# Four stacked graph layers on one core: weight sums moved to VectorE, and a new order of work in the first and the last group

## The chip, the cores and the metric

The kernel runs on one core of a Trainium2 chip. The metric is device time in microseconds (us), the median of three runs: 2460.32 us before the change (2459.33 to 2461.46). The profile is one further execution of the same kernel, with a span of 2456.7 us.

Engines are named as in the profile: PE is TensorE (matmul) and PEld its weight loads, DVE is VectorE, ACT is ScalarE, POOL is GpSimd, SP is SyncE, which here issues every transfer.

## The reference, cut to what matters

There are 128 graphs of 128 nodes with 512 features each, in 32-bit floats. Four layers follow each other, and each ends in a residual addition and a layer norm over the features:

```python
x = layernorm(x + relu(An @ x @ K0 + b0))                        # An = d^-1/2 (A + I) d^-1/2
x = layernorm(x + softmax_nodes(sum_m(q k^T / 8 * A)) * (x @ Wv^T))
x = layernorm(x + relu(concat(x, (A @ x) / deg) @ W2^T))
x = layernorm(x + An @ (x @ W3 + b3))
```

Every layer therefore has a product of a 128 x 512 matrix with one or two 512 x 512 weights for each graph, and layers 0, 2 and 3 have an aggregation with the graph's 128 x 128 matrix as well.

## The kernel before, in words

**Tiling.** The 128 graphs are worked on in 32 groups of G = 4. In a group the graphs form pairs: q is the pair (0 or 1) and r is the row in the pair, so graph 2q + r. Two graphs stacked, r = 0 over r = 1, form the left operand of a 2 x 2 block product whose right operand is a weight, also cut into 2 x 2 blocks. The product is done in Strassen-Winograd form with seven block products instead of eight. They are named B11, T1, B21, B22, T2, T3 and T4 (line 30). `project` (line 526) runs them in the order B11, B21, T1, T2, B22, T3; T4 is a "tail" that is put off until the next product's B11 has run (`finish_tails`, line 522). For some layers B21 comes after T1 (`early=False`).

**Sums ahead of the products.** T1 to T4 need sums of blocks. For a weight they are made once in the program (`weight_sums`, line 372: four operations of 128 x 512). For a left operand they are made for each group (`left_sums`, line 503: four operations named s1, s2, a21 and s4 below, on GpSimd as a rule). B11, B21 read blocks as they are. B22 reads s4, T1 reads s1, T2 reads s2, T3 the changed a21.

**Accumulation.** B11 and B21 share one PSUM region (g), T1 and B22 another (q), T2, T3 and T4 a third (v). When a second product is added onto a region, it must wait until the reader of the first is done: B21 waits for ScalarE's copy of B11 (`s_o`), B22 waits for VectorE's `u5 = q + sb` (written `u_o` in the profile).

**Transposes and aggregates.** `aggregate` (line 465) multiplies the features of one graph with the turned adjacency (four matmuls into a PSUM tile p_agg), and ScalarE copies the result out as the left operand. The normalised x of a layer is turned for the next product either through DRAM (`turn_x`, middle groups) or on TensorE (`turn_on_tensor`, line 489, for the first and last groups: a ScalarE copy, four transposes p_xT, a ScalarE copy back). `prep_rows` (line 411) scales the adjacency on VectorE; `prep_transpose` (line 436) turns it on TensorE for groups 0 and 1, and `prep_turn` (line 447) through DRAM for the rest.

**Order of the work.** The program is recorded first and then put in order by a planner (`Plan.schedule`, line 197). TensorE's order is the order of recording, exactly. On all other engines an instruction's place follows from a due time (the latest time at which TensorE's order needs it, counted backwards) and from estimated durations (`estimate`, line 292). What is recorded where, through `hooks` that run behind a named product, so sets TensorE's order directly and the other engines' order through the due times. At run time each engine works through its queue in order.

`begin` (line 847) writes out the first groups by hand: adjacency of group 0, layer 0 of groups 0 and 1, layer 1 of both, layer 2 of group 0, and so on. The loop at line 881 then interleaves layer 0 and 1 of group t with layer 2 and 3 of group t - 1. From line 898 on the last group's layers 2 and 3 are done pair by pair.

**Norms.** `norm_stats` (line 622) takes mean and variance with VectorE's batch-norm statistics, then GpSimd raises the variance to the power -1/2 and makes the products, and ScalarE applies scale and shift. `norm_last` (line 601) is the same for layer 3 with ScalarE doing the sums; only the very last row (last group, r = 1, pair 1) takes `norm_stats`. Each normalised graph of the last group is stored by a transfer of its own.

Of the kernel before, what the change touches and what calls it, by code (L numbers as in the profile page):

```python
# [10 lines left out]
FP = mybir.dt.float32  # L11
AF = mybir.ActivationFunctionType
ALU = mybir.AluOpType
AX = mybir.AxisListType

P = 128
K = 32
Q = P // K
G = 4
F = 512  # L20
# [291 lines left out]
def kernel(  # L312
# [59 lines left out]
    def weight_sums(w, eng):  # L372
        eng.tensor_tensor(w[:, :, T3], w[:, :, B22], w[:, :, T1], ALU.subtract)
        eng.tensor_tensor(w[:, :, T1], w[:, :, T1], w[:, :, B11], ALU.subtract)
        eng.tensor_tensor(w[:, :, T2], w[:, :, B22], w[:, :, T1], ALU.subtract)
        eng.tensor_tensor(w[:, :, T4], w[:, :, B21], w[:, :, T2], ALU.subtract)
# [59 lines left out]
    def prep_transpose(t):  # L436

        anT, arT, ana, d = prep_tiles(t)
        for i, done in ((0, lambda p: nc.vector.tensor_tensor(anT, p, per_graph(d), ALU.mult)),
                        (1, lambda p: nc.scalar.copy(arT, p))):  # L440
            p = ps_t.tile([P, G, P], FP, tag="pt", name=f"p_a{i}_{t}")
            with nc.unit():
                for g in range(G):
                    nc.tensor.transpose(p[:, g, :], ana[:, i, g, :], ident)
            done(p)
# [155 lines left out]
    def norm_last(name, t, r, pairs):  # L601

        z = st["x", t]
        qs = slice(pairs[0], pairs[-1] + 1)
        sm, nm, sq, rstd, nmr = (sp.tile([P, 2], FP, tag=f"last{i}", name=f"last{i}_{t}_{r}", bufs=2) for i in range(5))
        for q in pairs:
            row = tp.tile([P, F], FP, tag="row", name=f"row_{t}_{r}_{q}", bufs=1)
            nc.scalar.activation(row, z[:, 2 * q + r, :], AF.Copy, accum_out=sm[:, q:q + 1])
        nc.scalar.mul(nm[:, qs], sm[:, qs], -1.0 / F)
        for q in pairs:  # L610
            row = tp.tile([P, F], FP, tag="row", name=f"square_{t}_{r}_{q}", bufs=1)
            nc.scalar.activation(row, z[:, 2 * q + r, :], AF.Square, bias=nm[:, q:q + 1], accum_out=sq[:, q:q + 1])
        nc.gpsimd.tensor_scalar(rstd[:, qs], sq[:, qs], 1.0 / F, LN_EPS, ALU.mult, ALU.add)
        nc.gpsimd.tensor_tensor(rstd[:, qs], rstd[:, qs], nhalf[:, qs], ALU.pow)
        nc.gpsimd.tensor_tensor(nmr[:, qs], nm[:, qs], rstd[:, qs], ALU.mult)
        for q in pairs:
            zg = z[:, 2 * q + r, :]
            nc.scalar.activation(zg, zg, AF.Identity, bias=nmr[:, q:q + 1], scale=rstd[:, q:q + 1])
            if t == last:
                nc.sync.dma_start(out[t * G + 2 * q + r], zg)  # L620

    def norm_stats(name, t, r, pairs):
        if name == "o3" and (t, r, pairs[-1]) != (last, 1, 1):
            return norm_last(name, t, r, pairs)
        z = st["x", t]
        qs = slice(pairs[0], pairs[-1] + 1)
        mv = sp.tile([P, 2, 2], FP, tag="mv", name=f"mv{name}_{t}_{r}")
        for q in pairs:
            s = sp.tile([P, 6], FP, tag="bn", name=f"bn{name}_{t}_{r}_{q}")
            nc.vector.bn_stats(s, z[:, 2 * q + r, :])  # L630
            nc.vector.bn_aggr(mv[:, q, :], s)
        rstd = sp.tile([P, 2], FP, tag="rstd", name=f"rstd{name}_{t}_{r}")
        mr = sp.tile([P, 2], FP, tag="mr", name=f"mr{name}_{t}_{r}")
        nmr = sp.tile([P, 2], FP, tag="nmr", name=f"nmr{name}_{t}_{r}")
        nc.gpsimd.tensor_scalar(rstd[:, qs], mv[:, qs, 1], LN_EPS, None, ALU.add)
        nc.gpsimd.tensor_tensor(rstd[:, qs], rstd[:, qs], nhalf[:, qs], ALU.pow)
        nc.gpsimd.tensor_tensor(mr[:, qs], mv[:, qs, 0], rstd[:, qs], ALU.mult)
        nc.scalar.mul(nmr[:, qs], mr[:, qs], -1.0)
        for q in pairs:
            zg = z[:, 2 * q + r, :]  # L640
            nc.scalar.activation(zg, zg, AF.Identity, bias=nmr[:, q:q + 1], scale=rstd[:, q:q + 1])
            if name == "o3":
                nc.sync.dma_start(out[t * G + 2 * q + r], zg)


    def l0_agg(t, eng=nc.gpsimd, pairs=(slice(0, 2),)):
        left("agg0", t)
        for g in range(G):
            aggregate("agg0", t, g, st["anT", t])
        left_sums("agg0", t, eng, pairs)  # L650
# [7 lines left out]
    def l0_out(t, hooks=None, pairs=(0, 1)):  # L658
        fin = relu_add(t, pairs)

        def bias(h):
            return b0_sb[:, None, h * H:(h + 1) * H].to_broadcast([P, len(pairs), H])

        def first(p, block):
            sa, sb = copy_first(p, block)[0], block("sb")
            nc.gpsimd.tensor_tensor(sb, sa, bias(1), ALU.add)
            nc.gpsimd.tensor_tensor(sa, sa, bias(0), ALU.add)
            return sa, sb

        def c11(p, block):  # L670
            c = block("u2")
            nc.vector.tensor_tensor(c, p, bias(0), ALU.add)
            fin(0, 0, c)

        project("o0", t, [("agg0", w0_sb)], first, c11, fin, hooks, pairs=pairs)
# [111 lines left out]
    def l2_agg(t, r):  # L787
        if r == 0:
            left("agg2", t)
        for g in (r, 2 + r):  # L790
            aggregate("agg2", t, g, st["arT", t])
        if r == 1:
            left_sums("agg2", t)

    def l2_both(t, r):

        if r == 0:
            left("xT2", t)
            left("agg2", t)
        for g in (r, 2 + r):  # L800
            aggregate("agg2", t, g, st["arT", t])
        turn_on_tensor("xT2", t, r)
        if r == 1:
            left_sums("xT2", t, nc.vector)
            left_sums("agg2", t, nc.vector)

    def l2_out(t, hooks=None, pairs=(0, 1)):
        fin = relu_add(t, pairs)
        project("o2", t, [("xT2", w2x_sb), ("agg2", w2a_sb)],
                copy_first, lambda p, b: fin(0, 0, p), fin, hooks, pairs=pairs)  # L810
# [8 lines left out]
    def l3_agg_pair(t, q, eng):  # L819
        left(f"agg3{q}", t)  # L820
        for g in (2 * q, 2 * q + 1):
            aggregate(f"agg3{q}", t, g, st["anT", t])
        left_sums(f"agg3{q}", t, eng, ONE_BY_ONE[q:q + 1])
# [23 lines left out]
    def begin():  # L847

        prep_rows(0)
        prep_transpose(0)  # L850
        weight_sums(w0_sb, nc.gpsimd)
        l0_agg(0, nc.vector, ONE_BY_ONE)
        prep_rows(1)
        l0_out(0, {B21: [lambda: prep_transpose(1)], B22: [lambda: l0_agg(1)]})
        weight_sums(wv_sb, nc.vector)
        for w in (w2x_sb, w2a_sb, w3_sb):
            weight_sums(w, nc.gpsimd)

        l0_out(1)
        l1_turn(0, turn_on_tensor, (0,))  # L860
        finish_tails()
        l1_turn(0, turn_on_tensor, (1,))
        l1_out(0, {T3: [lambda: l1_turn(1, turn_on_tensor)]})
        l1_out(1, {B11: [lambda: l1_scores(0)], T1: [lambda: l1_softmax(0)], B21: [lambda: l1_add(0)]})
        l2_both(0, 0)
        l2_out(0, {B21: [lambda: l2_both(0, 1), lambda: prep(2)], T2: [lambda: l1_scores(1)], B22: [lambda: l1_softmax(1)], T3: [lambda: l1_add(1)]})
        l0_agg(2)
        l2_turn(1)
        l0_out(2, {B21: [lambda: l2_agg(1, 0)], T1: [lambda: l2_agg(1, 1)]})
        l3_agg(0)  # L870
        l3_bias(0)
        l3_out(0)

    def prep(t):
        if t < NT:
            load(t)
            prep_rows(t)
            prep_turn(t)

    begin()  # L880
    for t in range(2, NT):
        u = t - 1
        if t > 2:
            l0_out(t, {B21: [lambda: l2_agg(u, 0)], T1: [lambda: l2_agg(u, 1)]})
        tails.append(lambda: l1_turn(t))
        prep(t + 1)
        l2_out(u)
        if t < last:
            l0_agg(t + 1)
        l1_out(t, {})  # L890
        l3_agg(u)
        l1_scores(t)
        l3_bias(u)
        l3_out(u, {B11: [lambda: l1_softmax(t)], B21: [lambda: l1_add(t)]})
        if t < last:
            l2_turn(t)
# [1 line left out]
    l2_both(last, 0)  # L898
    held = tails.pop()
    for q in range(2):  # L900
        l2_out(last, {B21: [lambda: l2_both(last, 1), held]} if q == 0 else {}, (q,))
    for q in range(2):
        l3_agg_pair(last, q, nc.gpsimd)
        l3_bias(last, (2 * q, 2 * q + 1))
        l3_out(last, None, f"agg3{q}", (q,))
    finish_tails()
# [32 lines left out]
```

## Time and profile before

| what | value |
|---|---|
| device time, median of 3 | 2460.32 us |
| span of the profile | 2456.7 us |
| PE busy | 2436.3 us (99%) |
| DVE, POOL, ACT busy | 1711.2, 1341.0, 994.7 us |
| one middle group | 75.49 us of PE work |
| TensorE's granted clock | 0.999 |
| bytes read and written | 126.62 and 112.20 MB, 97 GB/s |

All instructions of the kernel carry line 271, since a recorder issues them; groups are told apart by their tiles. `p_o` is the PSUM of a projection, `p_v` of layer 1's product, `p_agg` of an aggregation, `p_xT` of a transpose of x, `p_a` of the adjacency. `w_sb` is the weight of layer 0 or of layer 3, `w2x_sb` and `w2a_sb` the two halves of layer 2's. A name with an s behind it (`agg0s`, `xT2s`, `agg30s`) is a left sum. `s_o` and `u_o` are blocks on their way from PSUM to x. `rstdo`, `mro`, `nmro` and `last` are the small columns of a norm.

In a timeline's line the first number is the start in us from the span's start, the second the time from there to the end of the last of the merged instructions. The bracket is how long the engine was idle before, and what ended that. In the list of waits the three numbers are the total in us, the count and the longest. Not all idle time of an engine costs something: here it is TensorE's idle time that does, and the time behind its last product.

### The profile page before, as it was taken

To read this page: it belongs to the slowest core of one execution; us is meant where nothing else is said; L and a number is where in the kernel's file an instruction comes from. 1 tells how busy PE (TensorE), PEld (TensorE's weight loads), DVE (VectorE), ACT (ScalarE), POOL (GpSimd) and SP (SyncE) were. 2 spreads that over 40 slices of the span, in tenths; PEclk is the share of its full clock that TensorE was granted. 3 is DMA by queue.
4 is the path that set the end of the run, shared out by engine and by line. 5 is a ranking of instruction groups with operands and counts; after the bars stand their busy time and mean duration, and the time that the engine had idled before them with its cause. 6 is when DMAs were issued, how large, how long until landed. Compare 5 with 4: busy or idle time off the path is not lost.

```text
span 2456.7 us, 35481 instructions
## 1 busy us (share of the span) xinstructions
PE 2436.3 (99%) x12462; PEld 2091.5 (85%) x12462; DVE 1711.2 (70%) x3389; ACT 994.7 (40%) x2120; POOL 1341.0 (55%) x1586
## 2 busy tenths in 40 slices
PE   8999999999999999999999999999999999999998
PEld 7788888888888888888888888888888888888887
DVE  6676776767667677676776667767677676776665
ACT  3344334444334443344433444433444334444335
POOL 6365555546455565555555554645555555555443
PEclk9999999999999999999999999999999999999999
DMA  5143243442434424244332444334443334432320
GB/s 176 27 124 85 76 107 108 124 111 61 113 90 125 125 68 109 74 127 122 86 91 83 124 116 108 71 101 103 116 125 72 88 90 125 125 99 64 82 70 35
DMA packets 393265, 241.14 MB, mean 98 GB/s; under 512 B 140416, under 2 KB 358016, under 8 KB 393088
## 3 DMA queue, kind: packets, MB, share of 16 engines
q1 hardware_dynamic: 393088, 238.88, 36.5%
q8 instruction: 99, 1.62, 0.3%
q14 instruction: 78, 0.64, 0.1%
HBM read 126.62 MB, written 112.20 MB: 97 GB/s over the span
## 4 chain that ended last, share of the span: by engine, by line
PE 97%; DVE 1%; ACT 1%; POOL 0%; DMA 0%; issue 0%; SPq 0%; ACTq 0%; POOLq 0%; DVEq 0%
PE p_o L271 62%; PE p_v L271 20%; PE p_agg L271 14%; PE p_sc L271 1%; DMA ana<-in_adj_dram 0%; DVE agg0s L271 0%; PE p_ws L271 0%; DVE x L271 0%; PE p_xT L271 0%; ACT xT L271 0%; PE p_w L271 0%; DVE ana L271 0%; ACT x L271 0%; DVE u_o L271 0%; SPq L271 0%
## 5 line engine op out<-in xcount | busy, mean ns | idle before, releaser
L271 PE MATMUL p_o<-w_sb,agg 128*128 128x256 f32 x2048 | 471.5, 380 | 1.6 <-DVE u_o L271 0.9
L271 PEld LDWEIGHTS p_o<-w_sb,agg 128*128 128x128 f32 x2048 | 386.4, 190 | 53.2 <-ACT s_o L271 1.1
L271 ACT COPY agg<-p_agg 128x512 f32<-128x512 f32 (+1 forms) x415 | 222.9, 552 | 456.2 <-PE p_agg L271 456.2
L271 PE MATMUL p_v<-wv_sb,xT 128*128 128x320 f32 x1024 | 291.4, 433 | 0.0
L271 DVE TENSOR_TENSOR v<-p_v,v 128x320 f32<-128x320 f32 x316 | 154.7, 490 | 173.1 <-PE p_v L271 170.6
L271 PE MATMUL p_o<-w2x_sb,xT 128*128 128x256 f32 x1024 | 263.3, 380 | 1.7 <-ACT s_o L271 1.1
L271 PE MATMUL p_o<-w2a_sb,agg 128*128 128x256 f32 x1024 | 262.9, 379 | 0.0
L271 PEld LDWEIGHTS p_v<-wv_sb,xT 128*128 128x128 f32 x1024 | 192.3, 190 | 75.8 <-issue 0.2
L271 PEld LDWEIGHTS p_agg<-anT,x 128*128 128x128 f32 x2048 | 238.7, 192 | 7.0 <-DVE anT L271 0.6
L271 PE MATMUL p_agg<-anT,x 128*128 128x128 f32 x2048 | 239.4, 275 | 0.3 <-DVE anT L271 0.3
L271 POOL TENSOR_TENSOR xT1s<-xT 128x512 f32<-128x512 f32 x32 | 45.5, 1423 | 351.1 <-DVE xT L271 250.0
L271 PEld LDWEIGHTS p_o<-w2x_sb,xT 128*128 128x128 f32 x1024 | 194.4, 190 | 32.4 <-ACT s_o L271 1.9
L271 PE MATMUL p_v<-wv_sb,xT1s 128*128 128x320 f32 x768 | 217.5, 433 | 0.1
L271 PEld LDWEIGHTS p_o<-w2a_sb,agg 128*128 128x128 f32 x1024 | 194.8, 190 | 26.1
L271 DVE TENSOR_TENSOR u_o<-p_o,u_o 128x512 f32<-128x512 f32 (+1 forms) x196 | 131.1, 670 | 118.2 <-PE p_o L271 118.1
L271 ACT ACTIVATE x<-x,nmro,rstdo 128x512 f32<-128x512 f32 x257 | 197.5, 808 | 4.5
L271 PE MATMUL p_o<-w2x_sb,xT2s 128*128 128x256 f32 x768 | 197.4, 380 | 1.5 <-DVE xT2s L271 1.5
L271 PE MATMUL p_o<-w2a_sb,agg2s 128*128 128x256 f32 x768 | 197.2, 379 | 0.0
L271 PEld LDWEIGHTS p_v<-wv_sb,xT1s 128*128 128x128 f32 x768 | 145.8, 190 | 57.5 <-POOL xT1s L271 0.6
L271 PE MATMUL p_o<-w_sb,agg0s 128*128 128x256 f32 x768 | 177.2, 380 | 3.5 <-DVE u_o L271 2.7
L271 PE MATMUL p_o<-w_sb,agg3s 128*128 128x256 f32 x744 | 173.9, 384 | 0.0
L271 DVE BATCH_NORM_STATS2 bno<-x 128x6 f32<-128x512 f32 x257 | 167.8, 683 | 3.4
(143 smaller groups left out, 4258.8 us busy)
## 6 DMA issues: line engine op xcount, KB each, us to landing
x<-in_x_dram SPq DMA_DIRECT2D x31, 1024.0 KB, 5.6
out_dram<-x SPq DMA_DIRECT2D x31, 1024.0 KB, 5.2
xT2s<-x SPq DMA_DIRECT2D x120, 256.0 KB, 2.5
xT2y<-xT2s SPq DMA_DIRECT2D x240, 128.0 KB, 3.3
xT1s<-x SPq DMA_DIRECT2D x120, 256.0 KB, 2.6
xT1y<-xT1s SPq DMA_DIRECT2D x240, 128.0 KB, 3.2
sa<-ana SPq DMA_DIRECT2D x120, 128.0 KB, 3.4
ya<-sa SPq DMA_DIRECT2D x120, 128.0 KB, 3.3
```

The costliest lines, as they stand in the source:

```text
L271: getattr(getattr(self.nc, op.engine), method)(*[v.real() if isinstance(v, Ref) else v for v in args], **{k: v.real() if isinstance(v, Ref ...
```

## The change

It has five parts.

1. The sums of layer 0's weight are made on VectorE instead of GpSimd.
2. In group 0's layer 0 the transposes of the second adjacency follow B11 instead of B21.
3. In group 0 and in the last group the second rows' aggregates and turned x for layer 2 follow that product's B11 instead of its B21, so that B21 stands between them and T1, which needs their sums. In the 29 middle groups (t > 2) the two halves of layer 2's aggregates each follow one product later of layer 0. Attention scores and softmax of group 1 are recorded one product sooner.
4. Pair 0's aggregates of the last layer 3 are recorded behind B22 of pair 1's layer 2, ahead of its T3, instead of after the whole product.
5. The last pair's normalisation is done on VectorE as (x - mean) x rstd, without the products that ScalarE's form needs, and the very last statistics are taken in two halves, the half that is finished first ahead.

```diff
@@ norm_last
-        nc.gpsimd.tensor_tensor(nmr[:, qs], nm[:, qs], rstd[:, qs], ALU.mult)
+        if (t, pairs[0]) != (last, 1):
+            nc.gpsimd.tensor_tensor(nmr[:, qs], nm[:, qs], rstd[:, qs], ALU.mult)
         for q in pairs:
             zg = z[:, 2 * q + r, :]
-            nc.scalar.activation(zg, zg, AF.Identity, bias=nmr[:, q:q + 1], scale=rstd[:, q:q + 1])
+            if (t, q) == (last, 1):
+                nc.vector.tensor_scalar(zg, zg, nm[:, q:q + 1], rstd[:, q:q + 1], ALU.add, ALU.mult)
+            else:
+                nc.scalar.activation(zg, zg, AF.Identity, bias=nmr[:, q:q + 1], scale=rstd[:, q:q + 1])
@@ norm_stats
         for q in pairs:
-            s = sp.tile([P, 6], FP, tag="bn", name=f"bn{name}_{t}_{r}_{q}")
-            nc.vector.bn_stats(s, z[:, 2 * q + r, :])
+            n = 2 if name == "o3" else 1
+            s = sp.tile([P, n, 6], FP, tag="bn", name=f"bn{name}_{t}_{r}_{q}")
+            for h in reversed(range(n)):
+                nc.vector.bn_stats(s[:, h], z[:, 2 * q + r, h * (F // n):(h + 1) * (F // n)])
             nc.vector.bn_aggr(mv[:, q, :], s)
...
         nc.gpsimd.tensor_tensor(rstd[:, qs], rstd[:, qs], nhalf[:, qs], ALU.pow)
+        if name == "o3":
+            zg = z[:, G - 1]
+            nc.vector.tensor_scalar(zg, zg, mv[:, 1, 0:1], rstd[:, 1:2], ALU.subtract, ALU.mult)
+            nc.sync.dma_start(out[B - 1], zg)
+            return
@@ begin
-        weight_sums(w0_sb, nc.gpsimd)
+        weight_sums(w0_sb, nc.vector)
         l0_agg(0, nc.vector, ONE_BY_ONE)
         prep_rows(1)
-        l0_out(0, {B21: [lambda: prep_transpose(1)], B22: [lambda: l0_agg(1)]})
+        l0_out(0, {B11: [lambda: prep_transpose(1)], B22: [lambda: l0_agg(1)]})
...
         l2_both(0, 0)
-        l2_out(0, {B21: [lambda: l2_both(0, 1), lambda: prep(2)], T2: [lambda: l1_scores(1)], B22: [lambda: l1_softmax(1)], T3: [lambda: l1_add(1)]})
+        l2_out(0, {B11: [lambda: l2_both(0, 1), lambda: prep(2)], T1: [lambda: l1_scores(1)], T2: [lambda: l1_softmax(1)], T3: [lambda: l1_add(1)]})
@@ the loop over groups
-            l0_out(t, {B21: [lambda: l2_agg(u, 0)], T1: [lambda: l2_agg(u, 1)]})
+            l0_out(t, {T1: [lambda: l2_agg(u, 0)], T2: [lambda: l2_agg(u, 1)]})
@@ the last group
-        l2_out(last, {B21: [lambda: l2_both(last, 1), held]} if q == 0 else {}, (q,))
+        l2_out(last, {B11: [lambda: l2_both(last, 1)], B21: [held]} if q == 0 else {B22: [lambda: l3_agg_pair(last, 0, nc.gpsimd)]}, (q,))
     for q in range(2):
-        l3_agg_pair(last, q, nc.gpsimd)
+        if q == 1:
+            l3_agg_pair(last, 1, nc.gpsimd)
```

More of the change, by code (lines that the diff above doesn't have):

```diff
@@ L641, in norm_stats @@
             nc.scalar.activation(zg, zg, AF.Identity, bias=nmr[:, q:q + 1], scale=rstd[:, q:q + 1])
-            if name == "o3":
-                nc.sync.dma_start(out[t * G + 2 * q + r], zg)
     def l0_agg(t, eng=nc.gpsimd, pairs=(slice(0, 2),)):
```

## The prediction

> **What bounds the kernel now.** I read the page's busy times first, then TensorE's waits, then the timelines of the stretches in which those waits lie. The page:
>
> ```profile
> PE 2436.3 (99%) x12462; PEld 2091.5 (85%) x12462; DVE 1711.2 (70%) x3389; ACT 994.7 (40%) x2120; POOL 1341.0 (55%) x1586
> ```
>
> TensorE is idle for 2456.7 - 2436.3 = 20.4 us of the span. The change alters no matmul in count or shape, so 20.4 us is all that it can win; a gain must come out of named gaps. TensorE's waits over the whole span:
>
> ```profile
> PE p_o L271 <- DVE u_o L271: 3.6, 3, 2.7
> PE p_o L271 <- ACT s_o L271: 1.8, 3, 0.7
> PE p_o L271 <- DVE xT2s L271: 1.5, 1, 1.5
> ...
> PE p_o L271 <- POOL agg30s L271: 1.3, 1, 1.3
> PE p_xT L271 <- ACT xT1y L271: 1.0, 1, 1.0
> PE p_o L271 <- DVE agg0s L271: 0.8, 3, 0.4
> ```
>
> With four smaller rows these make 12.3 us; the same view cut to 400 to 2300 us has no row at all, so the middle groups run without a gap, 75.49 us each in the chain. The other 7.9 us are the tail: TensorE ends at 2448.8. Where the waits lie, in TensorE's timeline (brackets: idle before, and who ended it; one more, 0.46 behind s_o, is at 2403.5):
>
> ```profile
> 15.17 2.00 PE L271 MATMUL p_o<-w_sb,agg 128*128 128x256 f32 x8 [0.68 <-ACT s_o L271]
> ...
> 25.97 1.99 PE L271 MATMUL p_o<-w_sb,agg0s 128*128 128x256 f32 x8 [2.74 <-DVE u_o L271]
> ...
> 91.25 1.13 PE L271 MATMUL p_o<-w2x_sb,xT 128*128 128x256 f32 x4 [0.68 <-ACT s_o L271]
> ...
> 99.13 1.13 PE L271 MATMUL p_o<-w2x_sb,xT2s 128*128 128x256 f32 x4 [1.50 <-DVE xT2s L271]
> ...
> 2437.30 1.13 PE L271 MATMUL p_o<-w_sb,agg30s 128*128 128x256 f32 x4 [1.31 <-POOL agg30s L271]
> ```
>
> In the first 26 us the late engine is VectorE. Its timeline, between GpSimd's weight sums and the addition that frees B22's bank:
>
> ```profile
> 12.99 1.75 DVE L271 TENSOR_TENSOR ana<-ana,d 128x512 f32<-128x512 f32 x1 [0.62 <-POOL d L271]
> ...
> 16.34 2.90 DVE L271 TENSOR_TENSOR agg0s<-agg 128x256 f32<-128x256 f32 x2
> ...
> 21.97 0.75 DVE L271 TENSOR_TENSOR agg0s<-agg,agg0s 128x256 f32<-128x256 f32 x2
> ...
> 25.23 1.28 DVE L271 TENSOR_TENSOR u_o<-p_o,sb_o 128x512 f32<-128x512 f32 x2
> ```
>
> ```profile
> 12.92 4.62 POOL L271 TENSOR_TENSOR w_sb<-w_sb 128x512 f32<-128x512 f32 x3
> ```
>
> See that two 256-wide additions take 2.90 us while GpSimd adds and 0.75 us as soon as it stops (21.8).
>
> [...] 1.45 us for one 256-wide addition beside GpSimd, 0.37 alone. [...]
>
> **Part A, the start.** w0's four sums leave GpSimd and become four 512-wide VectorE additions, 0.61 us from start to start (xT2s and agg2s at 2409.7 to 2412.1). The transposes of the second adjacency come behind B11 and not B21, 0.9 us of TensorE work that can lie under the 0.68 wait. Addressed: 0.68 + 0.22 + 0.37 + 0.21 (the three agg0s waits) + 2.74 = 4.22 us.
> VectorE from 12.99 on[...]: two row scalings 1.3, weight sums 4 x 0.61 = 2.4, six agg0s additions of 0.34 = 2.0, anT 0.6, the freeing addition 0.6: 6.9, so it would end at 19.9. The B21 addition, its residual add and the last two agg0s stood ahead of it before; if they still do, 2.0 more: 21.9. GpSimd's two bias adds (1.45 each) must run in that time, and can block VectorE for 0 to 2.9. So B22 starts between 21.75 (25.97 less all 4.22) and 24.8. I take 23.0, the 21.9 with somewhat under half of the blocking[...]: **3.0 us**, bounds 1.2 and 4.2. The new wait is that the transposes now stand ahead of B21: they need both row scalings, 12.99 + 1.3 = 14.3, and B11 ends at 14.5, so nothing if the scalings go first, up to 2 if weight sums are put before them; B21, T1, T2, B22 queue behind.
>
> **Part B, first group of layer 2.** Aggregates and turned x of the second rows go from behind B21 to behind B11. Their 1.8 + 0.9 us cover ScalarE's copy of the first product (0.68 wait). B21's 3.46 us (four runs of 0.865) then cover what follows the transposes, the xT copy and the first sum: 1.50 us, from 97.63 to 99.13. The inputs are there: x of those rows is normalised and turned at 89.96, B11 ends at 90.6. Moving scores and softmax of the second group one product forward costs nothing: its v was done at 86.0. **2.2 us.**
>
> **Part C, the 29 middle groups.** Aggregates move one product (1.73 us) back. TensorE's work is the same. GpSimd's sums, queued in order, start later:
>
> ```profile
> 1052.78 1.36 POOL L271 TENSOR_TENSOR agg2s<-agg 128x512 f32<-128x512 f32 x1 [4.59 <-ACT agg L271]
> ...
> 1059.91 1.59 POOL L271 TENSOR_TENSOR xT2s<-xT 128x512 f32<-128x512 f32 x1
> ```
>
> ```profile
> 1065.73 1.03 PE L271 MATMUL p_o<-w2x_sb,xT2s 128*128 128x256 f32 x4
> ```
>
> xT2s's first sum ends at 1061.5, and T1 wants it at 1065.7: 4.2 us of slack, 2.5 after the shift. On the other side x of the rows was ready 0.9 us ahead of its aggregates and gets 2.6. **0 us.**
>
> **Part D, the last group.** (1) Second rows behind B11: the 0.46 wait is covered, but ScalarE is full from 2400.3 to 2405.6 and TensorE also needs its copies for the transposes. 0 to 0.46; I take **0.3**. (2) Pair 0's layer-3 aggregates come before T3 of pair 1, 1.73 us sooner. Before, GpSimd's third agg30s sum stood behind a variance that arrived at 2435.3. Now four sums of 0.73 plus 1.6 of norms, from 2429.7, end near 2434, and B22 is due at 2436.0. **1.3.** x for pair 0 is ready at 2424.6, so nothing waits in exchange.
> (3) The tail:
>
> ```profile
> 2449.78 0.69 DVE L271 BATCH_NORM_STATS2 bno<-x 128x6 f32<-128x512 f32 x1
> ...
> 2450.90 0.22 POOL L271 TENSOR_SCALAR rstdo<-mvo 128x1 f32<-128x1 f32 x1
> ...
> 2452.31 0.81 ACT L271 ACTIVATE x<-x,nmro,rstdo 128x512 f32<-128x512 f32 x1
> 2453.03 0.80 ACT L271 ACTIVATE x<-x,last,last 128x512 f32<-128x512 f32 x1
> ```
>
> Two ScalarE normalisations follow each other to 2453.83. After the change half the statistics are taken early (0.69 becomes some 0.42, as other 256-wide operations), two small products vanish (0.19 and 0.20 with their hops), and both normalisations are VectorE's, the first under GpSimd's last power. GpSimd is held by the other graph's power to 2450.82 as before, so its own power ends at 2451.8; one normalisation at [...] 0.69 (nearest row): 2452.2 to 2452.5. That is 1.3 to 1.6, and up to 2.1 if GpSimd takes the last graph first. I take **1.4**. The store of 2.9 us stays.
>
> Sum: 3.0 + 2.2 + 0 + 0.3 + 1.3 + 1.4 = 8.2; 2460.3 - 8.2 = **2452.1 us**.
>
> **Rivals.** (i) The start stays VectorE's: it gets 2.4 us more to do, and if the planner puts weight sums ahead of the scalings, the new wait eats the gain. A 0.5, D1 0, tail 1.0: 0.5 + 2.2 + 1.3 + 1.0 = 5.0, 2455.3. For it: VectorE is the late engine already[...]. (ii) A transfer takes the early gain back: the third group's adjacency goes through DRAM and could hold its aggregates where they are; only D is left, 2457.3. Against it: its anT is done at 105.5 and read at 114.3, 8.8 us of slack for a shift of 5.2. (iii) Slower: the planner reorders and each of 29 groups waits 0.5 us for GpSimd's sums: 14.5 - 8.2, 2466.6. Against it: the 2.5 us of slack; for it: due times of the whole plan hang on this order, and a small wait is paid 29 times.
>
> **How the numbers follow.** Forecast 0.60, (i) 0.20, (ii) 0.10, (iii) 0.10. The range's low end takes the upper bounds, 4.2 + 2.2 + 0.5 + 1.3 + 2.1 = 10.3, and 0.7 for the xT1y wait that a new order may shrink: 2449.3. The high end takes in (i) and most of the slow side of its costs: 2457.0; (iii) and part of (ii) stay outside. Faster by over 0.2% is below 2455.4: the forecast and six tenths of (i), 0.72; slower 0.10; the rest 0.18.
>
> **What would show it.** Right: B22's wait near 26 us under 1.5; no xT2s wait near 96 us; a middle group still of 75.49 us with no row in TensorE's waits; no agg30s wait; 3.4 to 3.7 us from TensorE's end to the last normalisation's end, 5.0 before. Wrong: a wait of TensorE for ana or p_a's input near 15 us, any repeating row in the middle, or the last power on GpSimd delayed.

## The result, and the profile after

The changed kernel takes **2451.60 us** (median of 6 runs, 2451.41 to 2452.46) beside 2459.62 us for the kernel before in the same series (6 runs, 2457.69 to 2461.46): ratio 0.9968, 95% interval 0.9955 to 0.9981. Forecast: 2452.1. The spans of the two profiles differ by less than the medians, 2456.7 against 2449.8, 6.9 us. The section on the hardware comes back to the rest. Of all executions in this document one, of the kernel with the later softmax below, ran in a slower state (2820.89 us at a granted clock of 0.85) and is left out.

The page after, busy times:

```profile
PE 2437.9 (100%) x12462; PEld 2087.3 (85%) x12462; DVE 1714.5 (70%) x3396; ACT 996.4 (41%) x2117; POOL 1316.0 (54%) x1580
```

The matmuls are as many as before, yet PE is busy 1.6 us longer: the first hint that something is lost inside what counts as busy time. TensorE's waits after, over the whole span:

```profile
PE p_warm L271 <- POOL ident masks.py:199: 1.3, 1, 1.3
PE p_o L271 <- DVE u_o L271: 1.3, 3, 0.5
PE p_o L271 <- ACT xT L271: 1.0, 2, 0.7
PE p_v L271 <- POOL xT1s L271: 0.6, 1, 0.6
...
```

The waits add up to 4.8 us instead of 12.3; the first, ahead of the warm-up matmuls at the very start, is in both. Those behind xT2s, agg30s, s_o and agg0s are gone, and as before no row lies in the middle. TensorE's timeline after, at the places shown of before:

```profile
20.36 1.99 PE L271 MATMUL p_o<-w_sb,agg0s 128*128 128x256 f32 x8 [0.35 <-DVE u_o L271]
...
91.17 1.03 PE L271 MATMUL p_o<-w2x_sb,xT2s 128*128 128x256 f32 x4
...
2429.70 3.00 PE L271 MATMUL p_o<-w_sb,agg30s 128*128 128x256 f32 x12
```

The first B22 starts 5.61 us sooner, not the 3.0 that were forecast. But the end shows less than this start promises. Taking one landmark per group, the start of the score matmuls p_sc, and subtracting after from before gives the changed kernel's lead:

| landmark | before, us | after, us | lead, us |
|---|---|---|---|
| group 0's scores | 69.47 | 64.05 | 5.42 |
| group 2's scores | 199.30 | 191.07 | 8.23 |
| group 16's scores | 1256.20 | 1250.49 | 5.71 |
| group 31's scores | 2385.03 | 2381.46 | 3.57 |
| start of the last four matmuls | 2447.69 | 2441.95 | 5.74 |
| end of the last normalisation | 2453.83 | 2446.81 | 7.02 |

The start wins 8.2 us, the middle loses 4.7, the end wins 2.2 in TensorE's work and 1.2 behind it. Of 28 groups that took 75.49 us before, 25 now take 75.63 or 75.64 and three take 75.77, 76.03 and 75.79, and no list of waits shows it. What shows it is the chain of work that ended last (start, length, what), at p_w, the matmul that turns the score weights. One group's score matmuls p_sc and its p_w in the chain before, and then after:

```profile
1029.89 0.84 PE p_sc L271 x8
...
1032.51 0.11 PE p_w L271
```

```profile
1023.76 0.84 PE p_sc L271 x8
...
1026.38 0.25 PE p_w L271
```

p_w takes up 0.25 us of the chain and not 0.11. Its operand comes from VectorE, which first multiplies and sums what p_sc has left (scr). VectorE's timelines there, before and then after:

```profile
1026.76 0.68 DVE L271 TENSOR_TENSOR ana<-ana,ident 128x512 f32<-128x512 f32 x1
1027.36 2.49 DVE L271 SCALAR_TENSOR_TENSOR x<-b_sb,rs,x 128x512 f32<-128x512 f32 x3
1030.77 0.28 DVE L271 SCALAR_TENSOR_TENSOR scr<-p_sc,dmn,v 128x64 f32<-128x64 f32 x1 [0.91 <-PE p_sc L271]
```

```profile
1023.64 1.76 DVE L271 TENSOR_TENSOR ana<-ana,ident 128x512 f32<-128x512 f32 x1
1025.32 0.27 DVE L271 SCALAR_TENSOR_TENSOR scr<-p_sc,dmn,v 128x64 f32<-128x64 f32 x1
```

and GpSimd's after:

```profile
1023.57 1.28 POOL L271 TENSOR_TENSOR agg3s<-agg 128x512 f32<-128x512 f32 x1 [8.85 <-ACT agg L271]
```

See three things. Before, an operation on the next group's adjacency (ana) stands ahead of the bias additions, and VectorE is idle for 0.91 us when the scores (scr) arrive: there is slack. After, the planner has put an ana operation right ahead of the scores, on VectorE's queue with nothing between. It starts 0.07 us after a GpSimd addition (1023.64 and 1023.57) and ends 0.55 us after that one (1025.40 and 1024.85): 1.76 us instead of 0.68, the lengthening beside GpSimd that the prediction had measured in the first 26 us. The scores start with no idle time ahead of them, 1.56 us after the start of p_sc where it was 0.88 (1025.32 - 1023.76, 1030.77 - 1029.89). They are 0.68 us late. TensorE has other matmuls to do ahead of p_w, which hide most of that; p_w is late by 0.15 us.

The list of waits has no row for it, because TensorE's idle time is what lies between the end of one matmul and the start of the next, and those ends are modelled: in this group no idle time at all is recorded ahead of p_w, though it starts 0.15 us later. In the three slower groups a further 0.1 to 0.4 us goes in the same way, at p_w in one and behind a left sum of layer 1 (xT1s) in the two others; why just there is open.

### The profile page after: what moved, and what is told of

The parts are those of the page before. It is cut to its first block, busy times and chain, and to the rows that moved or that the text cites. A ratio compares the mean times of both kernels' runs of the same rounds, so it can differ in the third digit from the quotient of the medians.

```text
span 2449.8 us, 35470 instructions
## 1 busy us (share of the span) xinstructions
PE 2437.9 (100%) x12462; PEld 2087.3 (85%) x12462; DVE 1714.5 (70%) x3396; ACT 996.4 (41%) x2117; POOL 1316.0 (54%) x1580
## 4 chain that ended last, share of the span: by engine, by line
PE 96%; DMA 1%; DVE 1%; POOL 1%; SPq 0%; issue 0%; ACT 0%; POOLq 0%; DVEq 0%
PE p_o L271 61%; PE p_v L271 20%; PE p_agg L271 14%; PE p_sc L271 1%; SPq L271 0%; DMA x<-in_x_dram 0%; PE p_w L271 0%; DVE x L271 0%; DMA xT1s<-x 0%; DVE u_o L271 0%; PE p_ws L271 0%; DMA xT1y<-xT1s 0%; PE p_xT L271 0%; POOL xT2s L271 0%; DMA xT2y<-xT2s 0%
## 5 line engine op out<-in xcount | busy, mean ns | idle before, releaser
L271 POOL TENSOR_SCALAR rstdo<-mvo 128x2 f32<-128x2 f32 (+1 forms) x131 | 35.7, 272 | 320.9 <-DVE mvo L271 318.3
```

What stands on the lines that cost most here:

```text
L271: getattr(getattr(self.nc, op.engine), method)(*[v.real() if isinstance(v, Ref) else v for v in args], **{k: v.real() if isinstance(v, Ref ...
```

## The experiments

Each run is beside the kernel before on the same chip. **Set one**, four kernels; the kernel before had 2459.47 us.

**The changed kernel without part C**, to ask whether moving the aggregates back cost the middle its time.

```diff
-            l0_out(t, {T1: [lambda: l2_agg(u, 0)], T2: [lambda: l2_agg(u, 1)]})
+            l0_out(t, {B21: [lambda: l2_agg(u, 0)], T1: [lambda: l2_agg(u, 1)]})
```

> The changed kernel with the middle groups' aggregates back where they were (part C undone). Theory 1: part C's new due times let the planner put one row operation of the next adjacency right ahead of the score operations on VectorE[...], and p_w waits 0.15 us in each of 28 groups. Then a middle group is 75.49 us again, from scores to p_w 2.62 us, and the time is 2451.6 - 4.2 = 2447.4 us. Theory 2: the drift comes from the other parts (earlier start, other due times at the ends); then the group stays at 75.63 and the time at 2451.6. Theory 3: part C pays for something elsewhere (x ready later than its aggregates); then undoing it gives new waits of p_agg and the time is above 2451.6.

Measured: 2451.94 us (2451.69 to 2452.94), ratio 0.9972 (0.9961 to 0.9983): the same as with part C. The lead falls from 8.20 to 3.12 us within five groups (3 to 7) and then stays, at 75.49 us a group. In TensorE's waits there is a new row:

```profile
PE p_agg L271 <- ACT x L271: 2.5, 5, 0.5
```

In these five groups, and no others, the planned order has an ana operation right ahead of the scores. Late scores make a late softmax, late x, and aggregates that wait for x by 0.5 us: 0.9 to 1.3 us lost per group. Part C lets the aggregates come later, so the same fault costs 0.15 us; but with part C the fault is in 28 groups. The theory that C alone was the cause fell.

**The changed kernel with group t's softmax and v-addition two products later** in layer 3 of the group before.

```diff
-        l3_out(u, {B11: [lambda: l1_softmax(t)], B21: [lambda: l1_add(t)]})
+        l3_out(u, {T1: [lambda: l1_softmax(t)], T2: [lambda: l1_add(t)]})
```

> The changed kernel with part C kept, but softmax recorded behind T1 instead of B11 of layer 3's product and the addition of attention behind T2 instead of B21, so that p_w comes 1.73 us later and cannot wait for the scores. Theory 1 (the 0.15 us is p_w's wait for VectorE's scores, and nothing else): a middle group is 75.49 us and the time about 2447.5. Rival (the wait is lost somewhere else in the group, or the planner's order behind it makes a new one): 75.6 or more, 2451 or more.

Measured: median of eight 2452.64 us (2450.77 to 2454.34), ratio 0.9973 (0.9963 to 0.9983). Groups take 75.49 us up to group 27's scores, and eight of them do so with an ana operation right ahead of the scores, so p_w was the wait. But the next two groups take 77.98 and 75.98, with waits of up to 1.3 us (xT1s) and 0.6 us (xT2s), and the last group has one of 2.1 us (u_o): what comes behind softmax is now late. Nothing won.

**Part C alone** on the kernel before (the first diff, turned round).

> The kernel before with part C alone. Theory 1 in its strong form (part C by itself makes the p_w wait): 75.63 us a group, 2459.6 + 4.2 = 2463.8 us. Theory 1 in its weak form (part C only together with the other parts gives that order on VectorE; here the planned order differs): between 75.49 and 75.63, 2459.6 to 2463.8. Theory 2: no change, 2459.6.

Measured: 2460.35 us (2457.78 to 2461.20), ratio 1.0003 (0.9995 to 1.0011). No group has an ana operation ahead of its scores, and groups take 75.49 us (one 76.37, with a wait of 0.6 us behind xT1s). Part C by itself gains and loses nothing that this interval can tell; that one group apart, it does not bring the loss in the middle.

**Part A alone** on the kernel before.

```diff
-        weight_sums(w0_sb, nc.gpsimd)
+        weight_sums(w0_sb, nc.vector)
...
-        l0_out(0, {B21: [lambda: prep_transpose(1)], B22: [lambda: l0_agg(1)]})
+        l0_out(0, {B11: [lambda: prep_transpose(1)], B22: [lambda: l0_agg(1)]})
```

> The kernel before with part A alone: weight sums of layer 0 on VectorE and the second adjacency's transposes behind B11. By the prediction 3.0 us less, 2456.6. By the trace of the changed kernel 5.4 us less by the first scores, 2454.2, of which up to 1.9 from the second adjacency's load going ahead of the weight (lands at 8.7 us, not 10.6). Rival: the lead is lost again in the middle groups through a changed order on VectorE, 2457 to 2459.

Measured: 2455.93 us (2455.00 to 2457.04), ratio 0.9985 (0.9978 to 0.9991). The lead is 5.22 at the first scores, 4.70 at group 2 and 2.55 from group 5 on; three groups with the ana operation ahead of the scores lose it, as in the first run.

**Set two**; the kernel before had 2459.91 us.

**The changed kernel with a higher price for ana operations in the planner.** This leaves every instruction of the program alone, and TensorE's order too; it changes the order on the other engines: `estimate` counts 300 ns more for an operation on ana, 1.03 us for an addition and not 0.73, nearer to the 1.76 us measured beside GpSimd, so that the planner places it earlier.

```diff
-    return 160 + (1.12 if len(both) > 1 else 1.04) * n, 0, 0, len(both) > 1
+    slow = 300 if isinstance(out, Ref) and out.tile.args[3]['name'].startswith('ana') else 0
+    return 160 + (1.12 if len(both) > 1 else 1.04) * n + slow, 0, 0, len(both) > 1
```

> The changed kernel with one edit in the planner's estimates: VectorE's row additions and scalings of an adjacency count 300 ns more, which moves them away from the place right ahead of the score operations in all 28 groups (in the planned order none stands there; 28 did). No instruction is added or removed. Theory 1 (a row operation ahead of the scores[...] delays p_w by 0.15 us a group): 75.49 us a group, 2451.6 - 4.6 = 2447.0 us. Rival (the drift has another cause, such as the lead itself running into a transfer): 75.6 us, 2451.6.

Measured: **2446.92 us** (2446.56 to 2447.73), ratio 0.9950 (0.9937 to 0.9962), the lowest median of all kernels here. All groups take 75.49 us and the lead stays at 7.58 us from group 3 to 31. VectorE's timeline in this kernel, same place:

```profile
1019.18 0.68 DVE L271 TENSOR_TENSOR ana<-ana,ident 128x512 f32<-128x512 f32 x1
1019.78 2.49 DVE L271 SCALAR_TENSOR_TENSOR x<-b_sb,rs,x 128x512 f32<-128x512 f32 x3
1023.19 0.28 DVE L271 SCALAR_TENSOR_TENSOR scr<-p_sc,dmn,v 128x64 f32<-128x64 f32 x1 [0.91 <-PE p_sc L271]
```

The ana operation is back in its old place, takes 0.68 us, and the scores have their 0.91 us of slack again. With it the loss in the middle went. The new price also moved other work, on VectorE, ScalarE, GpSimd and in the order of the transfers, so this run alone does not single out the ana operation. The traces taken together do. From group 2 on, in all kernels of this document but the one with the later softmax, 40 groups have an ana operation right ahead of the scores. It takes 1.75 or 1.76 us in each of them, and p_w starts 0.14 to 0.51 us later behind p_sc than it does elsewhere. In the other 350 groups p_w starts at the same distance behind p_sc, within 0.01 us. With the two steps between, ana late and scores late, seen in the timelines, the cause is shown.

**Weight sums alone** on the kernel before (the first line of part A's diff).

> The kernel before with the weight sums of layer 0 on VectorE and nothing else. No row operation stands ahead of scores in the middle groups of this plan. Theory A1 [...]: B22 of the first group starts 2.5 to 3 us earlier, 2456.5 to 2457. Theory A2 (the second adjacency's earlier load and transposes are worth most): at most 1 us, 2458.5 or more, as VectorE gets 2.4 us more to do.

Measured: 2454.78 us (2454.22 to 2455.52), ratio 0.9980 (0.9973 to 0.9987). B22 starts at 22.40 after a wait of 0.81, and every group takes 75.49 us. The lead in the profile is 3.08 us; the medians differ by 5.1, since the profiled execution of the kernel before (2458.50 us) lies 1.4 below its median here and that of this kernel (2455.48) lies 0.7 above.

**Earlier transposes alone** on the kernel before (the second line of that diff).

> The kernel before with the second adjacency's transposes behind B11 and nothing else; its load now goes out ahead of both halves of layer 0's weight. One group of this plan has a row operation ahead of the scores (0.9 us). Theory A1: [...]B22 gains 0.7 (the covered wait) to 1.5 us, 2459 or so. Theory A2: B22 gains 2 to 3 us, 2457.5 or less.

Measured: 2458.65 us (2456.40 to 2460.22), ratio 0.9996 (0.9988 to 1.0004). The second adjacency lands 2.1 us sooner (VectorE's first use of it at 8.53 us, 10.60 before), since the earlier use makes the planner issue its load ahead of the weight's two halves and no longer between them; B22 starts at 23.93 instead of 25.97, after a wait of 3.80 us. Nearly nothing of that arrives at the end: one group of 75.80 us, and a lower clock at 24 to 30 us (0.82, 0.50 and 0.82 in stages of 2 us, last section).

**Part D alone** on the kernel before: the last group's order and the last normalisation.

> The kernel before with part D alone: the last group's new order and the normalisations on VectorE. The prediction: 0.3 + 1.3 + 1.4 = 3.0 us less, 2456.5. By the traces of the whole change 2.2 us of TensorE's end and 1.2 us of the tail, 2456.1. Rival (the end's gain needs the other parts): 2458 or more.

Measured: 2456.45 us (2454.21 to 2457.86), ratio 0.9986 (0.9980 to 0.9993). TensorE's waits in the last group are those of the changed kernel: nothing behind agg30s, 0.68 behind xT, 0.52 ahead of the last product. From group 31's scores to the end of the last normalisation it is 3.45 us faster than the kernel before, and so is the changed kernel: the end's gain needs no other part.

**Set three**; the kernel before had 2460.09 us.

**Part B alone** on the kernel before.

```diff
-        l2_out(0, {B21: [lambda: l2_both(0, 1), lambda: prep(2)], T2: [lambda: l1_scores(1)], B22: [lambda: l1_softmax(1)], T3: [lambda: l1_add(1)]})
+        l2_out(0, {B11: [lambda: l2_both(0, 1), lambda: prep(2)], T1: [lambda: l1_scores(1)], T2: [lambda: l1_softmax(1)], T3: [lambda: l1_add(1)]})
```

> Part B alone on the kernel before. Theory 1 (part B takes away TensorE's waits behind s_o and xT2s in the first group of layer 2, 0.68 + 1.50 us, and their restarts, and the planned order gets a row operation right ahead of the scores in two groups): 2.8 us won at group 2, 0.3 to 1.8 us given back in two groups, no further loss; 2457.4 to 2458.4 us. The wait of 2.74 us ahead of the first B22 stays. Theory 2 (B's gain is given back in later groups whatever the order): 2459.5 us, with the lead draining over many groups.

Measured: 2459.02 us (2457.32 to 2460.51), ratio 0.9995 (0.9987 to 1.0004), a little above the range that was expected for theory 1. Part B wins 2.87 us in its own stage (the lead goes from -1.97 at the first scores to 0.90 at group 2) and two groups of 76.41 and 76.40 us, the two with the ana operation ahead of the scores, take 1.83 of it back. The -1.97 comes from a later landing (0.5) and a lower clock from 26 us on (0.88, 0.50 and 0.77 in the three stages of 2 us to 32 us, 1.00 in the profile of the kernel before).

**The kernel with dearer ana operations, and part C undone as well.**

> The changed kernel with row operations priced 300 ns dearer in the planner, as in the run before that did this, and with part C undone as well (layer 2's aggregates behind B21 and T1 again). Theory 1 (the whole loss in the middle came from the row operation ahead of the scores; where the aggregates stand is then worth nothing): every group 75.49 us, no wait behind x at the aggregates, 2446.9 us, the same as with part C. Theory 2 (part C is of use by itself, since the aggregates otherwise reach x too early): a wait of 0.3 to 0.5 us of aggregates on x in many groups, 2450 us or more.

Measured: 2447.74 us (2447.41 to 2447.99), ratio 0.9949 (0.9936 to 0.9961) beside 0.9950 with part C. All groups take 75.49 us and there is no wait of aggregates for x. Where the aggregates stand is worth nothing as soon as VectorE's order is good.

**The kernel with dearer ana operations, and D1 undone**: the last group's second rows behind B21 again.

> The changed kernel with row operations priced 300 ns dearer, and with the last group's second rows of layer 2 behind B21 again (part D1 undone). Theory 1 (D1 exchanges three waits of 0.21, 0.24 and 0.46 us near 2400 us for one of 0.68, so it is worth 0.2 to 0.4 us): 2447.2 us. Theory 2 (D1 brought the 0.57 us by which the end won more than was predicted): 2447.8 us or more.

Measured: 2448.19 us (2447.20 to 2448.66), ratio 0.9951 (0.9937 to 0.9964); the interval can't part it from the run with D1, the traces can. From group 31's scores to the last four matmuls it takes 61.28 us, with D1 60.50: D1 is worth 0.78 us.

**Set four**; the kernel before had 2459.70 us.

**The wait ahead of the first B22 filled** with matmuls that compute nothing of use, on the kernel before.

```diff
+    def warm_more():
+        p = ps_t.tile([P, C, P], FP, tag="pt", name="p_more")
+        for i in range(9):
+            nc.tensor.matmul(p[:, i % C, :], ident, ident, start=True, stop=True, skip_group_check=True)
...
-        l0_out(0, {B21: [lambda: prep_transpose(1)], B22: [lambda: l0_agg(1)]})
+        l0_out(0, {B21: [lambda: prep_transpose(1)], T2: [warm_more], B22: [lambda: l0_agg(1)]})
```

> The kernel before, with nine more matmuls of the identity by itself (the same as at the start, 0.21 us each, result unused) recorded behind T2 of the first group, so that they run in the wait ahead of the first B22. They leave the additions on VectorE and the start of B22 as they were. Theory 1 (the wait of 2.74 us itself lets TensorE's clock fall in most executions, which costs about 1.5 us): no execution below a mean clock of 0.999, the stage from 25 to 30 us at 1.00, and 2457.5 to 2458.5 us, with the narrow spread of the changed kernel. Theory 2 (the drop of the clock has another cause): mean clocks of 0.998 and a median of 2459.5 to 2460.5 us, as before. One planned row operation ahead of the scores can cost up to 0.9 us in either case.

Measured: 2458.63 us (2457.69 to 2459.30), ratio 0.9996 (0.9988 to 1.0005). The interval does not tell its median from the kernel before; the clock does. All 13 executions had a mean clock of 0.999, while 13 of the 17 of the kernel before beside it had 0.998 and one 0.997. From the landing of the second adjacency to B22 it takes 15.37 us, as in the kernel before. The last section draws on it.

## Why the prediction was right

The total was right within 0.5 us, and that is luck: two of its terms were off by more than 2 us in opposite directions. A, B and D together won 11.6 us and not 8.2, C lost 4.7 that were put at nothing, and the medians hold 1.1 us more than the profiles, which no term had. Of the prediction's own signs of being right, a middle group still of 75.49 us did not come. Each term in the profiles' own time, predicted and measured:

| step | predicted, us | measured, us | from |
|---|---|---|---|
| A, the start | 3.0 | 5.4 | lead at the first scores |
| B, first group of layer 2 | 2.2 | 2.8 | 8.23 - 5.42; alone 2.87 |
| C, the middle groups | 0 | -4.7 | 3.57 - 8.23 |
| D1, second rows | 0.3 | 0.8 | 61.28 - 60.50 |
| D2, agg30s | 1.3 | 1.4 | 5.74 - 3.57 - 0.78 |
| D3, the tail | 1.4 | 1.2 | 7.88 - 6.72 |
| sum | 8.2 | 6.9 | spans 2456.7 - 2449.8 |

The tail's two numbers are the time from the last product's end (2448.82 and 2443.08) to the span's.

**A** had the right mechanism for the sums; its size was wrong, and above the 4.2 us that the prediction held to be the most it could win. VectorE's timeline after:

```profile
11.12 0.69 DVE L271 TENSOR_TENSOR ana<-ana,d 128x512 f32<-128x512 f32 x1 [0.62 <-POOL d L271]
...
14.93 2.90 DVE L271 TENSOR_TENSOR agg0s<-agg0s,agg 128x256 f32<-128x256 f32 x2
...
19.63 0.67 DVE L271 TENSOR_TENSOR u_o<-p_o,sb_o 128x512 f32<-128x512 f32 x1
```

The prediction's sum can be read off here, term by term. It let the row scaling start at 12.99; it starts at 11.12, because the second adjacency landed 1.9 us sooner (10.60 to 8.72 us), as in the run with earlier transposes alone. That the new order would also reorder the loads was not considered; it is the larger part of the error. (Part of the 1.9 us is scatter: VectorE's first use lies between 9.54 and 11.08 us in the six kernels here with the old order of loads, between 8.41 and 9.44 in the eight with the new one.) The two scalings do go ahead of the weight sums (from 12.33), as was hoped. Beside GpSimd's two bias additions (14.58 to 17.55) VectorE lost 2.15 of the possible 2.9 us (the 2.90 row, 0.75 us for the next two additions of that size, with GpSimd idle); the prediction's share of somewhat under half was the author's estimate. Against that the planner left the fourth weight sum, the residual add and the last two agg0s behind the freeing addition: 19.9 + 0.6 (B21's addition) - 0.6 (the fourth sum) - 1.9 + 2.15 = 20.2; it ended at 20.30. From the landing to B22 it took 11.64 us and not 15.37: 3.7 us for the sums, 1.9 for the landing, together the 5.61. The runs bear out this split: in every kernel here with the sums on GpSimd that time is 15.36 to 15.40 us, in every one with the sums on VectorE 11.50 to 11.67. The transposes alone, at 15.40, won nothing there beyond the earlier landing, so covering the 0.68 us wait was worth nothing at B22.

**B** held: no wait for xT2s, none for s_o. It won 0.6 us beyond the two listed waits. A trace shows where that can lie: a wait that cost more than its listed idle time. The changed kernel without C has two neighbouring groups, one with a wait at its aggregates and one without:

```profile
516.05 1.89 PE L271 MATMUL p_o<-w_sb,agg0s 128*128 128x256 f32 x8
518.45 2.05 PE L271 MATMUL p_agg<-arT,x 128*128 128x128 f32 x16 [0.51 <-ACT x L271]
...
592.32 1.89 PE L271 MATMUL p_o<-w_sb,agg0s 128*128 128x256 f32 x8
594.05 1.95 PE L271 MATMUL p_agg<-arT,x 128*128 128x128 f32 x16
```

The aggregates start 2.40 us after the product ahead of them instead of 1.73, which is 0.67 for a listed wait of 0.51, and then take 0.10 longer: 0.27 us beyond the list. Two waits at that rate make 0.5 us (an estimate) of B's 0.6. The prediction's limits, 4.2 us for A and 20.4 in all, counted listed idle time only and were too low for this reason; for A, B11 also started 0.63 us sooner. (Its 12.3 us of waits and 7.9 of tail leave 0.2 of the 20.4 us without a place; nothing hangs on that.)

**C** is the step that failed: "TensorE's work is the same" and "0 us", where 4.7 us were lost. The slack was worked out for the engine whose queue the change was about, GpSimd's sums for T1, and it was indeed enough: no xT2s or agg2s wait came in any middle group. The loss came from VectorE, from an operation of the next group's adjacency that the change does not name. Rival (iii) came closest, a small wait paid in each middle group; it named the planner's reordering, but had the engine wrong and the size (0.5 us a group, where mostly 0.15 was lost). The planned orders settle it. The number of groups with an ana operation right ahead of the scores, and what was lost there:

| kernel | groups | lost, us |
|---|---|---|
| before; part C alone; sums alone; part D alone | 0 | none for this reason |
| transposes alone; wait filled | 1 | 0.3 |
| part B alone | 2 | 0.9 each |
| part A alone | 3 | 2.1 in all |
| changed, without C | 5 | 0.9 to 1.3 each |
| changed | 28 | 0.15 in 25, 0.3 to 0.5 in three |
| changed, softmax later | 8 | none in these, since the scores are used later |
| changed, ana dearer (with C, without C, without D1) | 0 | none |

Which due time moves the ana operation there was not isolated. What is shown is that the planner counts 0.73 us for an operation that takes 0.68 or 1.76, that a higher price moves it away, and that the loss goes with it. A, B, the transposes alone and even the filled wait each bring it about in one to three groups, C alone in none; only the whole change does so in nearly all.

**D1** was put at 0.3 and gave 0.8. Three waits (0.21, 0.24 and 0.46) did make way for one of 0.68 behind ScalarE's xT, as feared, which is 0.23 of recorded waiting; the remaining 0.55 fits what two waits fewer are worth beyond the list, 2 x 0.27 (an estimate). **D2** was as predicted. **D3** came in at 3.73 us from TensorE's end, for 3.4 to 3.7. The changed kernel's tail, GpSimd and then VectorE:

```profile
2444.86 0.22 POOL L271 TENSOR_SCALAR rstdo<-mvo 128x1 f32<-128x1 f32 x1 [0.40 <-DVE mvo L271]
2445.04 0.57 POOL L271 TENSOR_TENSOR last<-last,nhalf 128x1 f32<-128x1 f32 x1
2445.58 0.65 POOL L271 TENSOR_TENSOR rstdo<-rstdo,nhalf 128x1 f32<-128x1 f32 x1
```

```profile
2445.64 0.55 DVE L271 TENSOR_SCALAR x<-x,last,last 128x512 f32<-128x512 f32 x1 [0.87 <-POOL last L271]
2446.26 0.55 DVE L271 TENSOR_SCALAR x<-x,mvo,rstdo 128x512 f32<-128x512 f32 x1
```

The first normalisation does lie under GpSimd's last power, which ends at 2446.23; the second follows at once. It takes 0.55 us, less than the 0.69 that was counted at most; the low end of that forecast, 2452.2, was the author's estimate, and no trace of before showed it. One step went otherwise than predicted: the other graph's power ends 2.5 us after TensorE (2445.61 - 2443.08) and not 2.0 as before (2450.82 - 2448.82), because the planner put the small operation on VectorE's variance ahead of it, and GpSimd stood idle for 0.40 us.

## What to carry to other kernels

A change that is written as an order of one engine's work can alter the order of every other queue where a planner fills them from due times: after such a change compare the planned orders, not only the waits, and look for an operation that is slow, or that another engine's work lengthens (0.68 to 1.76 us here), and that has come to stand right ahead of a latency-critical one. A loss of 0.15 us a group is invisible in a list of waits; the lead of one kernel over the other, taken at one landmark per repetition, shows it at once and tells in which stage each gain was made and lost. A listed wait, too, can cost more than it shows: the one taken apart here cost 0.27 us more than its idle time. And a total that comes out right proves no term of the sum: here the middle gave back 4.7 of 8.2 us, and one price in the planner recovered it.

## What the runs showed of the hardware

**With a wait of 2.74 us ahead of the first B22, TensorE's granted clock fell in most executions.** The kernel before has that wait, and 96 of its 120 executions beside these runs had a mean clock of 0.998 or 0.997. In its own profile the granted clock stayed at 1.00 there; in that of part C alone, with the same wait, it was 0.66. One stage of that kernel (busy times of PE, PEld, DVE, ACT, POOL with counts, granted clock, DMA share, GB/s), and its B22:

```profile
25.00:30.00 5.00, 4.47 (x20) 3.88 (x21) 2.82 (x5) 0.16 (x1) 0.00 (x0) 0.66 1.05 307
```

```profile
25.53 3.38 PE L271 MATMUL p_o<-w_sb,agg0s 128*128 128x256 f32 x8 [2.74 <-DVE u_o L271]
```

B22 takes 3.38 us instead of 1.99. In finer stages of the run with earlier transposes alone:

```profile
24.00:26.00 2.00, 2.00 (x8) 1.72 (x9) 1.20 (x2) 0.00 (x0) 0.00 (x0) 0.82 0.88 227
26.00:28.00 2.00, 2.00 (x10) 1.91 (x10) 1.49 (x3) 0.00 (x0) 0.00 (x0) 0.50 1.07 277
28.00:30.00 2.00, 2.00 (x17) 2.00 (x17) 2.00 (x5) 1.17 (x2) 0.00 (x0) 0.82 1.04 276
```

The middle stage is at 0.50. If the clock was 0.50 in the whole of the low stretch (an estimate), the stretch lasted (0.18 + 0.50 + 0.18) x 2 / 0.50 = 3.4 us here, and 0.34 x 5 / 0.50 = 3.4 us in part C alone. By this estimate all of it comes after the wait is over here (B22 starts at 23.93, the half clock at about 25.3). In part C alone B22's 1.39 us more are 2.8 us of the stretch, and the aggregates behind it take 3.73 us, as in the profile of the kernel before, so the stretch sets in at about 25.0, half a microsecond before B22. The wait was 3.80 us in the one and 2.74 us in the other, and the same 2.74 us brought no drop in the profile of the kernel before.

The run with the filled wait shows that the wait is the cause: with at most 0.73 us of idle time left ahead of B22, none of 13 executions had less than 0.999, where 14 of 17 did beside it. All the executions compared of each kernel here that makes the sums on VectorE read 0.999 or 1.000 as well. The mean is too coarse to count every drop, though: the profiles of part C alone and of part B alone read 0.999 and show one.

What a drop costs can be estimated in two ways. From the medians it is 2459.70 - 2458.63 = 1.1 us, and 0.3 more that one late group lost in the filled kernel, so about 1.4 us, with the reserve that the interval of that ratio includes 1. The 120 executions of the kernel before beside these runs, sorted by their clock, average 2460.05 us at 0.998 (95 of them) and 2458.07 at 0.999 (24), 2.0 us apart. This would account for the medians of before and after differing by 8.0 us where the profiles differ by 6.9: the profile of the kernel before shows no drop, and its execution (2458.50 us) was 1.1 us faster than the median, while that of the changed kernel (2451.53) was at its median. So the change also took away a loss that the prediction, argued from one profile at full clock, could not know of.

**A VectorE addition beside a GpSimd addition, seen again:** 1.76 us for one of 128 x 512 with both inputs in SBUF, when it is issued 0.07 us after a GpSimd addition of 1.28 us, and 0.68 us while GpSimd is idle. The addition `v<-p_v,v` of 128 x 320, which reads PSUM, shows no such difference in the kernel before: it takes 0.49 us at 1015.66, beside a GpSimd addition from 1014.94 to 1016.21, and 0.49 us at 1024.20, with GpSimd idle.
